# Two graph layers on one core: laying out buffers by when they end, and issuing the second layer's first loads among the first layer's last gathers

## Chip, cores, metric

One core of one Trainium2 chip runs the whole kernel. The metric is the device time of one execution in microseconds; lower is better. Engines are named as in the profile: PE (matrix multiply), PEld (its weight load), DVE (vector), ACT (scalar), POOL, and SP, which here only issues DMAs.

## What is computed

```python
h = relu(layernorm(x))                       # x: 2500 x 1024
x = x + segment_sum((h @ W0)[src] * edge_weight[:, None], dst)   # 80000 edges, sorted by dst
h = relu(layernorm(x)) @ W1.T + b1
deg = 1 + count(row == n)                    # row = src, col = dst, and a self edge per node
x = x + segment_sum(deg[row]**-0.5 * deg[col]**-0.5 * h[col], row)
```

## The kernel before

Nodes lie in 20 tiles of 128 (`NT`); the last has 68. `ORDER` gives the order in which tiles are finished. Arithmetic follows three stages.

**Support.** Each x tile is normed and multiplied by W0 (L282); the rows of `support` are stored to device memory. Meanwhile DVE and PE count the edges between tiles (`count_group`, L442 to L466): `counts` tiles are stored as `cnat`, and `total` adds them up for the degrees.

**Layer 1.** For the four thickest tiles (0 to 3), a `dense` weighted count matrix is multiplied with rows of `support` (`multiplied`, L632). For the 16 others `gathered` fetches, block by block, 128 edge rows with an indirect DMA issued on POOL (L592, eight `msg` buffers), makes a one-hot `oh_r`, splits the weighted message into `hi` on ACT (L598) and `lo` on DVE (L600), and adds four matmuls into `sums` (L604). When a tile's blocks are done, `finish` adds x (L562), stores x1 (L563), norms it (`normed`, L133 to L145) and transposes it on PE (L546) with copies to `vT` on ACT (L547). Then `second_rows` multiplies with W1 (L577; the profile has two PE records for each fp32 matmul), adds `bias` (L581) and stores `hid_d` (L584). A plan written out in Python interleaves blocks, dense rows and pieces of `finish` and `second_rows`; after the plan's end what is left is run off: first `preparing` and `waiting` (the last tiles' `finish`), then `products_left` (their `second_rows`).

**Layer 2.** Degrees are reduced (L740) and `dis` made (L743); a flag `missing` is computed that says whether a general fallback has to run (L744 to L754; one matmul of `ones` and `placed`, L749). Then each `hid_d` tile is loaded (`rows`, three buffers, L764), scaled by `dis` and split into `hi` (ACT, L766) and `lo` (DVE, L768), all kept in SBUF for all 20 tiles. For each output tile r, `counts_of` loads a transposed column of `cnat` with a DMA transpose on SP (`cT`, L774) and casts it to fp32r on ACT (`bT`, L776, two buffers); 80 matmuls (L794) run over all tiles in `ORDER`. Rows 0 and 1 are done as a pair, so that each fresh `hi`/`lo` serves two rows; the rest one by one. `row` loads x1 (L781), adds (L782) and stores (L784).

A scheduler at build time orders the instructions of each engine; buffers of one name rotate in program order. `order_behind` adds an edge to that ordering only, with no semaphore. Pools are stacked: a pool opened after others are closed takes their bytes. With `reuse_waits="tile"` a tile of such a pool waits for the earlier users of its own bytes (in PSUM, of its own bank) only; otherwise it waits for all users of the pools below it. `lay2`, `work2` and `psum2` of layer 2 have this already. They begin where `lay` began, so `hi` and `lo` of the first tiles in `ORDER` lie on `lay`'s tiles, `bias` among them.

Of the kernel before, what the change touches and what calls it, by code (L numbers as in the profile page):

```python
# [9 lines left out]
F32 = mybir.dt.float32  # L10
F32R = mybir.dt.float32r
# [28 lines left out]
OPENING = 8  # L40
BESIDE = 12
TAIL = 48

ORDER = (3, 4, 5, 6, 2, 7, 8, 9, 1, 10, 11, 12, 13, 0, 14, 15, 16, 17, 18, 19)

# [2 lines left out]
def direct(  # L48
# [67 lines left out]


    first = ctx.enter_context(ExitStack())
    lay = first.enter_context(tc.tile_pool(name="lay", bufs=1))
    work = first.enter_context(tc.tile_pool(name="work", bufs=2))  # L120
    psum = first.enter_context(tc.tile_pool(name="psum", bufs=2, space=bass.MemoryType.PSUM))
    ohs = first.enter_context(tc.tile_pool(name="ohs", bufs=8))
    cpool = first.enter_context(tc.tile_pool(name="cpool", bufs=3))
    wpool = first.enter_context(tc.tile_pool(name="wpool", bufs=1, reuse_waits="tile"))
    sup_ctx = tc.tile_pool(name="sup", bufs=4, side="right")
    sup = sup_ctx.__enter__()
    prep_ctx = tc.tile_pool(name="prep", bufs=1)
# [158 lines left out]

    def products(t):
        hT, rstd = ready.pop(t)
        mm = psum.tile([P, 2, H], F32, name="mm")
        yield from product(hT, w0_sb, mm)  # L290
        row = sup.tile([P, D], F32, name="row", bufs=2)
        nc.scalar.activation(row, mm.rearrange("p h d -> p (h d)"), AF.Copy, scale=rstd)
        nc.sync.dma_start(support[t * P:t * P + rows(t), :], row[:rows(t), :])
# [138 lines left out]
    def count_group(t, g, a, b):  # L432

        nonlocal last_count
        w = WINDOWS[t][1]
        cleared(t)
        if g % 4 == 0:
            bases[t] = nc.values_load_multi_w_load_instructions(
                base_i[0:1, g:g + 4], engines=[DVE], min_val=0, max_val=P - w,
                skip_runtime_bounds_check_because="a row of a tile")[1]  # L440
        v = bases[t][g % 4]
        cb = psum.tile([P, 512], F32, name="cb")  # L442
        ab = []
        for k in range(a, b):
            oh_low = ohs.tile([P, P], BF, name="oh_low")
            nc.vector.tensor_scalar(oh_low, iota16[:, :P], low[:, k:k + 1], None, op0=ALU.is_equal)  # L446
            oh_key = ohs.tile([P, KW], BF, name="oh_key")
            nc.vector.tensor_scalar(oh_key[:, :NT * w], iota16[:, :NT * w], key[:, k:k + 1], None,  # L448
                                    op0=ALU.is_equal)
            last_count = nc.tensor.matmul(  # L450
                cb[:, :NT * w], oh_low, oh_key[:, :NT * w], start=(k == a), stop=(k == b - 1))
            if t < DENSE:
                wl = ohs.tile([P, 3, P], BF, name="wl")
                for i in range(3):
                    nc.scalar.activation(wl[:, i, :], oh_low, AF.Copy, scale=wpart[:, i, k:k + 1])  # L455
                ab.append((wl, oh_key))
        to = counts[t][:, :, ds(v, w)]
        nc.vector.tensor_tensor(to, cb[:, :NT * w].rearrange("p (t w) -> p t w", w=w), to, op=ALU.add)  # L458
        if t < DENSE:
            for j, (wl, oh_key) in enumerate(ab):  # L460
                for i in range(3):
                    last_count = nc.tensor.matmul(  # L462
                        cb[:, 256:256 + NT * w], wl[:, i, :], oh_key[:, :NT * w],
                                     start=(j == 0 and i == 0), stop=(j == len(ab) - 1 and i == 2))
            to = dense[t][:, :, ds(v, w)]
            nc.vector.tensor_tensor(to, cb[:, 256:256 + NT * w].rearrange("p (t w) -> p t w", w=w), to,  # L466
                                    op=ALU.add)
        if b == K0[t + 1]:
            nc.vector.tensor_tensor(total, counts[t], total, op=ALU.add)
            to_store.append([6, t])  # L470
# [100 lines left out]
    def second_rows(t, vT):  # L571
# [12 lines left out]
        nc.sync.dma_start(hid_d[t], hid)  # L584
        yield 1.75, 0.65, 0.0

    def gathered(t, sums):
        n = TILE_BLOCKS[t]
        for j in range(n):
            k = K0[t] + j  # L590
            msg = gpool.tile([P, D], F32, name="msg", bufs=8)
            nc.gpsimd.indirect_dma_start(  # L592
                out=msg, out_offset=None, in_=support,
                in_offset=bass.IndirectOffsetOnAxis(ap=src_p[:, k:k + 1], axis=0))
            oh = gpool.tile([P, P], F32R, name="oh_r", bufs=3)
            nc.vector.tensor_scalar(oh, iota, row_p[:, k:k + 1], None, op0=ALU.is_equal)  # L596
            hi = gpool.tile([P, D], F32R, name="hi")
            nc.scalar.activation(hi, msg, AF.Copy, scale=wgt_p[:, k:k + 1])  # L598
            lo = gpool.tile([P, D], F32R, name="lo")
            nc.vector.scalar_tensor_tensor(lo, msg, wgt_p[:, k:k + 1], hi.bitcast(F32),  # L600
                                           op0=ALU.mult, op1=ALU.subtract)
            for v in (hi, lo):
                for h in range(2):
                    i = nc.tensor.matmul(  # L604
                        sums[:, h, :], oh, v[:, h * H:(h + 1) * H],
                        start=(j == 0 and v is hi), stop=(j == n - 1 and v is lo))
                    if v is hi and h == 0:
                        on_pe(i)
            yield 0.92, 1.47, 1.16
# [3 lines left out]
    def multiplied(ts):  # L613
# [3 lines left out]
        for t in ts:  # L617
            count_all(t)
        for h in range(2):
            sums = psum.tile([P, 2, H], F32, name="mm")  # L620
            cols = slice(h * H, (h + 1) * H)
            for k0 in range(0, NT, 2):
                msg = gpool.tile([P, 2, H], F32, name="msg", bufs=8)
# [52 lines left out]
    def blocks_of(tiles):  # L676
        nonlocal pending
        for t in tiles:
            sums = psum.tile([P, 2, H], F32, name="mm")
            for j, took in enumerate(gathered(t, sums)):  # L680
                if j == TILE_BLOCKS[t] - 1:
                    rest = finish(t, sums)
# [46 lines left out]
            count_next(queue)  # L729
    store_counts(late=False)  # L730
    assert not stored
    for rest in [preparing] * (preparing is not None) + waiting:
        for _ in rest:
            pass
    for rest in products_left:
        for _ in rest:
            pass


    nc.vector.tensor_reduce(deg, total, axis=mybir.AxisListType.X, op=ALU.add)  # L740
    nc.vector.tensor_scalar(dis, deg, 1.0, None, op0=ALU.max)
    nc.scalar.activation(dis, dis, AF.Sqrt)
    nc.vector.reciprocal(dis, dis)  # L743
    nc.vector.tensor_reduce(placed[:, 1:2], deg, axis=mybir.AxisListType.X, op=ALU.add)  # L744
    over = lay.tile([P, NT], F32, name="over")
    nc.vector.tensor_scalar(over, deg, 2048.0, None, op0=ALU.is_gt)
    nc.vector.tensor_reduce(placed[:, 2:3], over, axis=mybir.AxisListType.X, op=ALU.add)
    ps = psum.tile([P, 4, P], F32, name="pT")
    nc.tensor.matmul(ps[:, 0, :3], ones, placed, start=True, stop=True)  # L749
    lost = lay.tile([1, 3], F32, name="lost")  # L750
    for i, n in enumerate((E, E + N, 0)):
        nc.vector.tensor_scalar(lost[:, i:i + 1], ps[0:1, 0, i:i + 1], float(n), None, op0=ALU.not_equal)
    nc.vector.tensor_add(lost[:, 0:1], lost[:, 0:1], lost[:, 1:2])
    nc.vector.tensor_add(missing, lost[:, 0:1], lost[:, 2:3])  # L754
    first.close()


    lay = ctx.enter_context(tc.tile_pool(name="lay2", bufs=1, reuse_waits="tile"))
    work = ctx.enter_context(tc.tile_pool(name="work2", bufs=2, reuse_waits="tile"))
    psum = ctx.enter_context(tc.tile_pool(name="psum2", bufs=2, space=bass.MemoryType.PSUM, reuse_waits="tile"))  # L760
    his, los = {}, {}
    for t in ORDER:
        hf = work.tile([P, D], F32, name="rows", bufs=3)
        nc.sync.dma_start(hf, hid_d[t])  # L764
        his[t] = lay.tile([P, D], F32R, name=f"hi{t}")
        nc.scalar.activation(his[t], hf, AF.Copy, scale=dis[:, t:t + 1])  # L766
        los[t] = lay.tile([P, D], F32R, name=f"lo{t}")
        nc.vector.scalar_tensor_tensor(los[t], hf, dis[:, t:t + 1], his[t].bitcast(F32),  # L768
                                       op0=ALU.mult, op1=ALU.subtract)

    def counts_of(r):

        cT = work.tile([P, NT, P], F16, name="cT")
        nc.sync.dma_start_transpose(out=cT.rearrange("p t s -> p (t s)"), in_=cnat[r].rearrange("t p d -> (t p) d"))  # L774
        bT = work.tile([P, NT, P], F32R, name="bT")
        nc.scalar.copy(bT, cT)  # L776
        return bT
# [1 line left out]
    def row(r, mm):  # L779
# [3 lines left out]
                                       op0=ALU.mult, op1=ALU.add)  # L783
        nc.sync.dma_start(out[r * P:r * P + rows(r), :], xh[:rows(r), :])  # L784


    for rs in [(0, 1)] + [(r,) for r in range(2, NT)]:
        bTs = [counts_of(r) for r in rs]
        mms = [psum.tile([P, 2, H], F32, name="mm2", bufs=3) for r in rs]
        for k in ORDER:  # L790
            for bT, mm in zip(bTs, mms):
                for v in (his[k], los[k]):
                    for h in range(2):
# [2 lines left out]
                                         stop=(k == ORDER[-1] and v is los[k]))  # L796
        for r, mm in zip(rs, mms):
            row(r, mm)


def kernel(tc, edges, xT, *args):
# [338 lines left out]
```

## Time and profile before

| | |
|---|---|
| median of 3 runs | 1740.54 us (1735.3, 1740.54, 1742.44) |
| profiled execution | 1733.96 us, its span 1732.0 us |
| PE, DVE, ACT, POOL busy | 96%, 69%, 52%, 30% of the span |
| mean granted PE clock | 0.988 |
| last gather issued, last gather matmul ends | 1287.18, 1316.9 us |
| last product (L577) ends | about 1345.9 us |
| pair of rows 0 and 1 (L794) | 1346.91 to 1391.82 us |
| rows 2 to 19 (L794) | 1393.82 to about 1722.9 us |

The profile's timeline lists instructions in order of time with, in brackets, the idle time of the engine before them and what ended it. The chain of waits follows what released each step back from the end. The windows view gives busy times in stretches.

### The profile page before, as it was taken

How to read it: one execution, taken by the hardware profiler on the slowest of the kernel's cores; microseconds unless marked ns; L12 is line 12 of the kernel's file. 1: busy time of each engine (PE TensorE's matmuls, PEld its weight loads, DVE VectorE, ACT ScalarE, POOL GpSimd, SP SyncE). 2: the span in 40 equal slices, each digit the busy share in tenths (PEclk: the TensorE clock that was granted, in tenths of full speed). 3: DMA queues.
4: the chain of work that ended last, by engine and by line, in shares of the span. 5: the costliest groups of instructions: out<-in, count | busy, mean ns of one | idle time of the engine just before them, and what ended most of it. 6: DMA issues, size and time to landing. Idle time of an engine off the chain costs nothing. (4 is left out here: it accounts for less than half of the span.)

```text
span 1732.0 us, 21214 instructions
## 1 busy us (share of the span) xinstructions
PE 1654.1 (96%) x6506; PEld 1030.8 (60%) x6506; DVE 1200.3 (69%) x3051; ACT 907.9 (52%) x1476; POOL 525.6 (30%) x501
## 2 busy tenths in 40 slices
PE   6999999999999999999999999998999899999997
PEld 2466555554445555655555555654564678888886
DVE  5788888888889999999999999996772510000000
ACT  3399999982236765665555556664553421111110
POOL 3000000000057776775555556664530000000000
PEclk9999999999999999999999999999999999999999
DMA  7512212123399999998988899898875663433320
GB/s 249 188 62 65 89 53 60 54 68 92 79 364 330 384 317 323 331 362 281 308 286 282 282 322 331 318 333 297 264 265 134 210 164 91 107 79 105 93 65 32
DMA packets 213584, 351.57 MB, mean 203 GB/s; under 512 B 115354, under 2 KB 134820, under 8 KB 213462
## 3 DMA queue, kind: packets, MB, share of 16 engines
q0 software_dynamic: 60592, 219.74, 36.2%
q1 hardware_dynamic: 152870, 130.39, 24.8%
q8 instruction: 54, 0.88, 0.2%
q14 instruction: 68, 0.56, 0.1%
HBM read 282.41 MB, written 54.56 MB: 195 GB/s over the span
## 5 line engine op out<-in xcount | busy, mean ns | idle before, releaser
L598 ACT ACTIVATE hi<-msg,wgt_p 128x1024 fp32r<-128x1024 f32 x378 | 428.6, 1149 | 280.6 <-PE mm L604 180.4
L592 POOL DMA_INDIRECT msg<-support,src_p x378 | 478.0, 1265 | 293.6 <-DVE oh_r L596 90.0
L600 DVE SCALAR_TENSOR_TENSOR lo<-msg,wgt_p,hi 128x1024 fp32r<-128x1024 f32 x378 | 480.1, 1277 | 36.7 <-ACT hi L598 21.1
L604 PE MATMUL mm<-lo,oh_r 128*128 128x512 f32 x756 | 309.8, 491 | 13.2 <-DVE lo L600 13.0
L282 PE MATMUL mm<-w,hT 128*128 128x512 f32 x640 | 318.4, 609 | 2.4 <-ACT hT L174 2.4
L577 PE MATMUL pT<-w,vT 128*128 128x512 f32 x640 | 312.4, 597 | 0.0
L604 PE MATMUL mm<-hi,oh_r 128*128 128x512 f32 x756 | 273.5, 442 | 0.7 <-ACT hi L598 0.7
L455 ACT ACTIVATE wl<-oh_low,wpart 128x128 bf16<-128x128 bf16 x891 | 262.2, 420 | 0.0
L794 PE MATMUL mm<-hi,bT 128*128 128x512 f32 (+1 forms) x800 | 247.6, 392 | 4.6 <-ACT bT L776 2.0
L794 PE MATMUL mm<-lo,bT 128*128 128x512 f32 (+1 forms) x800 | 247.7, 392 | 3.3 <-DVE lo L768 3.3
L782 DVE SCALAR_TENSOR_TENSOR rows<-mm,dis,rows 128x1024 f32<-128x1024 f32 x20 | 25.7, 1283 | 307.9 <-PE mm L794 307.8
L604 PEld LDWEIGHTS mm<-lo,oh_r 128*128 128x128 f32 x756 | 137.9, 189 | 129.3 <-DVE lo L600 51.1
L448 DVE TENSOR_SCALAR oh_key<-iota,key 128x200 bf16<-128x200 f16 (+12 forms) x675 | 194.4, 290 | 5.0 <-PE cb L462 4.9
L776 ACT CAST bT<-cT 128x2560 fp32r<-128x2560 f16 x20 | 46.6, 2335 | 261.0 <-PE mm L794 257.7
L604 PEld LDWEIGHTS mm<-hi,oh_r 128*128 128x128 f32 x756 | 139.3, 189 | 64.2 <-issue 30.2
L794 PEld LDWEIGHTS mm<-hi,bT 128*128 128x128 f32 (+1 forms) x800 | 150.4, 189 | 37.9 <-ACT hi L766 3.1
L794 PEld LDWEIGHTS mm<-lo,bT 128*128 128x128 f32 (+1 forms) x800 | 150.0, 188 | 38.3 <-DVE lo L768 7.0
L458 DVE TENSOR_TENSOR counts<-cb,counts 128x200 f32 (+13 forms) x296 | 138.5, 469 | 48.0 <-PE cb L450 41.2
L446 DVE TENSOR_SCALAR oh_low<-iota,low 128x128 bf16<-128x128 f16 x675 | 167.2, 251 | 1.4 <-ACT wl L455 1.2
L632 PE MATMUL mm<-msg,dense 128*128 128x512 f32 (+1 forms) x320 | 157.1, 601 | 10.2 <-DMA msg<-support 10.2
L577 PEld LDWEIGHTS pT<-w,vT 128*128 128x128 f32 x640 | 120.9, 191 | 72.6 <-issue 55.5
L282 PEld LDWEIGHTS mm<-w,hT 128*128 128x128 f32 x640 | 109.1, 195 | 65.4 <-issue 59.2
(144 smaller groups left out, 1177.5 us busy)
## 6 DMA issues: line engine op xcount, KB each, us to landing
msg<-support POOLq DMA_DIRECT2D x36, 512.0 KB, 6.8
xt<-in_x SPq DMA_DIRECT2D x34, 512.0 KB, 7.3
cnat<-counts SPq DMA_DIRECT2D x20, 640.0 KB, 5.4
hid_d<-hn SPq DMA_DIRECT2D x20, 512.0 KB, 6.5
rows<-hid_d SPq DMA_DIRECT2D x20, 512.0 KB, 4.4
rows<-x_d SPq DMA_DIRECT2D x20, 512.0 KB, 3.8
hT<-in_xT SPq DMA_DIRECT2D x19, 512.0 KB, 3.7
support<-row SPq DMA_DIRECT2D x19, 512.0 KB, 2.9
```

The source lines that it names most:

```text
L282: on_pe(nc.tensor.matmul(mm[:, h, :], vT[:, k, :], ws[k][:, h * H:(h + 1) * H], start=(k == 0), stop=(k == KC - 1)))
L446: nc.vector.tensor_scalar(oh_low, iota16[:, :P], low[:, k:k + 1], None, op0=ALU.is_equal)
L448: nc.vector.tensor_scalar(oh_key[:, :NT * w], iota16[:, :NT * w], key[:, k:k + 1], None, op0=ALU.is_equal)
L455: nc.scalar.activation(wl[:, i, :], oh_low, AF.Copy, scale=wpart[:, i, k:k + 1])
L458: nc.vector.tensor_tensor(to, cb[:, :NT * w].rearrange("p (t w) -> p t w", w=w), to, op=ALU.add)
L577: on_pe(nc.tensor.matmul(mm, vT[:, k, :], w1_sb[k][:, h * H:(h + 1) * H], start=(k == 0), stop=(k == KC - 1)))
L592: nc.gpsimd.indirect_dma_start(out=msg, out_offset=None, in_=support, in_offset=bass.IndirectOffsetOnAxis(ap=src_p[:, k:k + 1], axis=0))
L598: nc.scalar.activation(hi, msg, AF.Copy, scale=wgt_p[:, k:k + 1])
L600: nc.vector.scalar_tensor_tensor(lo, msg, wgt_p[:, k:k + 1], hi.bitcast(F32), op0=ALU.mult, op1=ALU.subtract)
L604: i = nc.tensor.matmul(sums[:, h, :], oh, v[:, h * H:(h + 1) * H], start=(j == 0 and v is hi), stop=(j == n - 1 and v is lo))
L632: m = nc.tensor.matmul(sums[:, i, :], dense[t][:rows(k), k, :], msg[:rows(k), k - k0], start=(k == 0), stop=(k == NT - 1))
L794: nc.tensor.matmul(mm[:, h, :], bT[:rows(k), k, :], v[:rows(k), h * H:(h + 1) * H], start=(k == ORDER[0] and v is his[k]), stop=(k == ORDE ...
```

## The change

The SBUF pools `lay`, `work`, `ohs` and `cpool` get `reuse_waits="tile"`, and `wpool` moves ahead of `ohs` and `cpool`. The PSUM pool is split in three: `psum_c` (the `cb` tiles), `psum_m` (the `mm` tiles) and `psum` (the `pT` tiles), in this order. In layer 2, `psum2` is opened first; then come a pool `late` with the hi/lo of the 11 tiles last in `ORDER`, in reverse order, `work2`, and a pool `early` with the hi/lo of the first `EARLY = 9`. Splitting a tile becomes a function, called inside the loop of the first pair; its load is ordered behind one of the last gathers, and so are the transposing loads of `cnat`. After the plan's end, `products_left` is run off first, then the unfinished `finish`, then `products_left` again. The flag's reductions, matmul and comparisons move behind row 4.

```diff
+EARLY = 9
-    lay = first.enter_context(tc.tile_pool(name="lay", bufs=1))
-    work = first.enter_context(tc.tile_pool(name="work", bufs=2))
+    lay = first.enter_context(tc.tile_pool(name="lay", bufs=1, reuse_waits="tile"))
+    work = first.enter_context(tc.tile_pool(name="work", bufs=2, reuse_waits="tile"))
+    psum_c = first.enter_context(tc.tile_pool(name="psum_c", bufs=2, space=bass.MemoryType.PSUM))
+    psum_m = first.enter_context(tc.tile_pool(name="psum_m", bufs=2, space=bass.MemoryType.PSUM))
     psum = first.enter_context(tc.tile_pool(name="psum", bufs=2, space=bass.MemoryType.PSUM))
-    ohs = first.enter_context(tc.tile_pool(name="ohs", bufs=8))
-    cpool = first.enter_context(tc.tile_pool(name="cpool", bufs=3))
     wpool = first.enter_context(tc.tile_pool(name="wpool", bufs=1, reuse_waits="tile"))
+    ohs = first.enter_context(tc.tile_pool(name="ohs", bufs=8, reuse_waits="tile"))
+    cpool = first.enter_context(tc.tile_pool(name="cpool", bufs=3, reuse_waits="tile"))
...
+    drawn = []
     def gathered(t, sums):
...
-            nc.gpsimd.indirect_dma_start(
+            drawn.append(nc.gpsimd.indirect_dma_start(
                 out=msg, out_offset=None, in_=support,
-                in_offset=bass.IndirectOffsetOnAxis(ap=src_p[:, k:k + 1], axis=0))
+                in_offset=bass.IndirectOffsetOnAxis(ap=src_p[:, k:k + 1], axis=0)))
...
-    for rest in [preparing] * (preparing is not None) + waiting:
-        for _ in rest:
-            pass
-    for rest in products_left:
-        for _ in rest:
-            pass
+    def exhaust(generators):
+        while generators:
+            for _ in generators.pop(0):
+                pass
+    exhaust(products_left)
+    exhaust([preparing] * (preparing is not None) + waiting)
+    exhaust(products_left)
...
-    lay = ctx.enter_context(tc.tile_pool(name="lay2", bufs=1, reuse_waits="tile"))
+    psum = ctx.enter_context(tc.tile_pool(name="psum2", bufs=2, space=bass.MemoryType.PSUM, reuse_waits="tile"))
+    late = ctx.enter_context(tc.tile_pool(name="late", bufs=1, reuse_waits="tile"))
+    his, los = {}, {}
+    def parts_of(t, pool):
+        his[t] = pool.tile([P, D], F32R, name=f"hi{t}")
+        los[t] = pool.tile([P, D], F32R, name=f"lo{t}")
+    for t in ORDER[:EARLY - 1:-1]:
+        parts_of(t, late)
     work = ctx.enter_context(tc.tile_pool(name="work2", bufs=2, reuse_waits="tile"))
-    psum = ctx.enter_context(tc.tile_pool(name="psum2", bufs=2, space=bass.MemoryType.PSUM, reuse_waits="tile"))
-    his, los = {}, {}
-    for t in ORDER:
+    early = ctx.enter_context(tc.tile_pool(name="early", bufs=1, reuse_waits="tile"))
+    for t in ORDER[:EARLY]:
+        parts_of(t, early)
+    def split(t):
         hf = work.tile([P, D], F32, name="rows", bufs=3)
-        nc.sync.dma_start(hf, hid_d[t])
-        his[t] = lay.tile([P, D], F32R, name=f"hi{t}")
+        order_behind(nc.sync.dma_start(hf, hid_d[t]), drawn[-max(12 - 4 * ORDER.index(t), 1)])
         nc.scalar.activation(his[t], hf, AF.Copy, scale=dis[:, t:t + 1])
-        los[t] = lay.tile([P, D], F32R, name=f"lo{t}")
...
     def counts_of(r):
         cT = work.tile([P, NT, P], F16, name="cT")
-        nc.sync.dma_start_transpose(out=cT.rearrange("p t s -> p (t s)"), in_=cnat[r].rearrange("t p d -> (t p) d"))
+        i = nc.sync.dma_start_transpose(out=cT.rearrange("p t s -> p (t s)"),
+                                        in_=cnat[r].rearrange("t p d -> (t p) d"))
+        order_behind(i, drawn[-max(30 - 12 * r, 1)])
...
     for rs in [(0, 1)] + [(r,) for r in range(2, NT)]:
...
         for k in ORDER:
+            if rs[0] == 0:
+                split(k)
...
         for r, mm in zip(rs, mms):
             row(r, mm)
+        if rs[0] == 4:
+            all_placed()
```

`all_placed()` holds L744 to L754 as they were, with its matmul in an `mm2` tile of `psum2` and its small tiles in `keep`.

More of the change, by code (lines that the diff above doesn't have):

```diff
@@ L288, in products @@
         hT, rstd = ready.pop(t)
-        mm = psum.tile([P, 2, H], F32, name="mm")
+        mm = psum_m.tile([P, 2, H], F32, name="mm")
         yield from product(hT, w0_sb, mm)
@@ L441, in count_group @@
         v = bases[t][g % 4]
-        cb = psum.tile([P, 512], F32, name="cb")
+        cb = psum_c.tile([P, 512], F32, name="cb")
         ab = []
@@ L619, in multiplied @@
         for h in range(2):
-            sums = psum.tile([P, 2, H], F32, name="mm")
+            sums = psum_m.tile([P, 2, H], F32, name="mm")
             cols = slice(h * H, (h + 1) * H)
@@ L678, in blocks_of @@
         for t in tiles:
-            sums = psum.tile([P, 2, H], F32, name="mm")
+            sums = psum_m.tile([P, 2, H], F32, name="mm")
             for j, took in enumerate(gathered(t, sums)):
@@ L743, in direct @@
     nc.vector.reciprocal(dis, dis)
[L744 to L754, printed above, removed]
-    first.close()
-    lay = ctx.enter_context(tc.tile_pool(name="lay2", bufs=1, reuse_waits="tile"))
+    first.close()
+    psum = ctx.enter_context(tc.tile_pool(name="psum2", bufs=2, space=bass.MemoryType.PSUM, reuse_waits="tile"))
[6 more added lines that the diff above has]
+        parts_of(t, late)
     work = ctx.enter_context(tc.tile_pool(name="work2", bufs=2, reuse_waits="tile"))
-    psum = ctx.enter_context(tc.tile_pool(name="psum2", bufs=2, space=bass.MemoryType.PSUM, reuse_waits="tile"))
-    his, los = {}, {}
-    for t in ORDER:
+    early = ctx.enter_context(tc.tile_pool(name="early", bufs=1, reuse_waits="tile"))
+    for t in ORDER[:EARLY]:
+        parts_of(t, early)
+    def split(t):
         hf = work.tile([P, D], F32, name="rows", bufs=3)
-        nc.sync.dma_start(hf, hid_d[t])
-        his[t] = lay.tile([P, D], F32R, name=f"hi{t}")
+        order_behind(nc.sync.dma_start(hf, hid_d[t]), drawn[-max(12 - 4 * ORDER.index(t), 1)])
         nc.scalar.activation(his[t], hf, AF.Copy, scale=dis[:, t:t + 1])
-        los[t] = lay.tile([P, D], F32R, name=f"lo{t}")
         nc.vector.scalar_tensor_tensor(los[t], hf, dis[:, t:t + 1], his[t].bitcast(F32),
@@ L784, in row, with all_placed @@
         nc.sync.dma_start(out[r * P:r * P + rows(r), :], xh[:rows(r), :])
+    def all_placed():
+        nc.vector.tensor_reduce(placed[:, 1:2], deg, axis=mybir.AxisListType.X, op=ALU.add)
+        over = keep.tile([P, NT], F32, name="over")
+        nc.vector.tensor_scalar(over, deg, 2048.0, None, op0=ALU.is_gt)
+        nc.vector.tensor_reduce(placed[:, 2:3], over, axis=mybir.AxisListType.X, op=ALU.add)
+        ps = psum.tile([P, 2, H], F32, name="mm2", bufs=3)
+        nc.tensor.matmul(ps[:, 0, :3], ones, placed, start=True, stop=True)
+        lost = keep.tile([1, 3], F32, name="lost")
+        for i, n in enumerate((E, E + N, 0)):
+            nc.vector.tensor_scalar(lost[:, i:i + 1], ps[0:1, 0, i:i + 1], float(n), None, op0=ALU.not_equal)
+        nc.vector.tensor_add(lost[:, 0:1], lost[:, 0:1], lost[:, 1:2])
+        nc.vector.tensor_add(missing, lost[:, 0:1], lost[:, 2:3])
     for rs in [(0, 1)] + [(r,) for r in range(2, NT)]:
```

## The prediction

> **What bounds the kernel now.** I first read the page's busy shares: PE is at 96% of 1732.0 us, so a change can only pay where PE stands still or runs slowly. The windows then show where that is.
>
> ```profile
> 1250.00:1300.00 50.00, 50.00 (x173) 30.48 (x172) 39.36 (x60) 30.39 (x32) 20.87 (x19) 1.00 0.77 259
> 1319.00:1336.00 17.00, 13.63 (x34) 6.69 (x35) 2.30 (x6) 8.40 (x7) 0.00 (x0) 0.90 0.97 237
> 1348.00:1392.00 44.00, 39.05 (x157) 28.47 (x157) 24.96 (x21) 20.93 (x19) 0.00 (x0) 1.00 0.73 234
> 1400.00:1450.00 50.00, 50.00 (x222) 41.35 (x221) 2.57 (x2) 4.67 (x2) 0.00 (x0) 1.00 0.40 108
> ```
>
> Columns: stretch, length, busy PE, PEld, DVE, ACT, POOL, clock, DMA share, GB/s. PE is full in the last gathers and again once layer 2 runs row by row; the loss lies in the seam, 1317 to 1394. The PE timeline there:
>
> ```profile
> 1316.74 1.88 PE L577 MATMUL pT<-w,vT 128*128 128x512 f32 x4
> 1322.37 1.55 PE L546 MATMUL pT<-ident,hn 128*128 128x128 f32 x8 [3.75 <-ACT hn L145]
> 1323.74 22.11 PE L577 MATMUL pT<-w,vT 128*128 128x512 f32 x48
> 1345.68 0.28 PE L749 MATMUL pT<-placed,ones 128*128 128x3 f32 x2
> 1346.91 0.93 PE L794 MATMUL mm<-hi,bT 128*128 128x512 f32 x3 [0.94 <-DVE lost L753]
> ...
> 1390.61 1.21 PE L794 MATMUL mm<-lo,bT 68*128 68x512 f32 x4
> 1393.82 0.73 PE L794 MATMUL mm<-hi,bT 128*128 128x512 f32 x2 [2.00 <-ACT bT L776]
> ```
>
> PE waits 3.75 us for the last tile's norm; then the 48 products run, 16 of which (the second half of tile 18) needed no such norm. The first pair of layer-2 rows takes 1391.82 - 1346.91 = 44.91 us. The chain of waits gives the unhindered rates:
>
> ```profile
> 1309.90 1.72 PE pT L577 x4
> 1349.50 5.00 DMA rows<-hid_d
> 1357.10 5.43 DMA rows<-hid_d
> 1366.24 4.00 DMA rows<-hid_d
> 1393.82 329.04 PE mm L794 x1440
> ```
>
> So a product record costs 0.43 us, a layer-2 matmul 329.04/1440 = 0.2285 us, and the pair's 160 would need 36.56 us: it loses 8.35 us, because three `rows` buffers reload only as each `lo` is done. Why nothing was split earlier is in the waits of 1290 to 1395:
>
> ```profile
> ACT hi L766 <- DMA rows<-hid_d: 20.8, 15, 3.6
> ACT hi L766 <- DVE hn L581: 13.1, 1, 13.1
> ```
>
> The second is a buffer wait: L581 reads `bias`, whose bytes in `lay` lie under the first `lo` and second `hi` of layer 2, and it runs last at 1345.89. Only one `hi` (1332.35) escaped. Similarly the first L794 waited for `lost` (L753), the last reader of a `pT` bank.
>
> **What the skill says.** The Trainium skill, "Perfetto Trace Analysis", section "Tensor Engine Instruction", calls ACT and DVE strict FIFO. The trace agrees: at 1206.27 DVE's stats (L133) had waited 7.52 us for a load, and PE, needing the `lo` behind it, stood 6.00 us until 1208.40. "DMA: Bandwidth & Descriptors", section "Issuing engines are not separate DMA queues", says transfers from all issuers share the same 16 engines; here four transposes and two row loads raised the share to 0.97 in 1319 to 1336. "TensorE: Matmul & The Clock Gate", section "What's actually happening", says an idle window of about 3.4 us throttles PE's clock until it has been busy again. The trace agrees: after the 3.75 us gap the clock column falls to 0.90, and 48 records take 22.11 us, not 20.64.
>
> **The change, part by part** (times of the profiled execution).
>
> *Order of the tail.* Tile 18's remaining 16 records (6.9 us) now come before tile 19's norm and transposes. DVE's stats need only tile 19's sums, so the chain of about 5.4 us (1316.94 to 1322.37) runs beside them. Gone: 3.75 us idle, the slow clock (22.11 - 20.64 = 1.47) and the slow transposes (1.55 - 2 x 0.44 = 0.67, less 0.18 of overlap). Saved: 5.7 us. Late next: the two vT copies of 0.59 us; the first half is copied while the second is transposed, so I take nothing for them; they could cost at most 1.2.
>
> *Places of buffers.* Nine of twenty hi/lo pairs (72 KB a partition) move to the far end, on bytes of `dense` and the gather's msg, hi and lo; the other eleven, of the tiles needed last, go on `lay`, `work` and the weights. Layer 2's PSUM falls on the cb and mm banks, not pT. Tiles 3, 4, 5 can then be split before the gathers end, the next ones as msg buffers end (last gather issued 1287.18), and all nine by about 1325; PE turns them into 9 x 1.83 = 16.4 us of work after about 1340. The eleven late ones wait for the weights, free when the products end. Three are preloaded; the reload pace was (1383.9 - 1348.3)/17 = 2.1 us a row, so the last is ready about 1340 + 4 + 8 x 2.1 = 1361, while PE asks for it at 1340 + 19 x 1.83 = 1375. The 8.35 us go. If the order puts early layer-2 matmuls ahead of the last products, the late eleven start up to 13 us later and up to 3 us come back.
>
> *Moved issues.* The transposes of rows 0, 1 and 2 go behind the 30th, 18th and 6th last gather (issued 1223.98, 1251.65, 1275.51), three row loads behind the 12th, 8th and 4th last (1263.40, 1271.80, 1280.11), the rest behind the last. All stay on SP; POOL gets none. A transpose holds SP 2.2 to 5.0 us; behind it there stand hid_d and x1 stores and L152's loads, which are issued at least 19 us before DVE uses them and land in about 7, so 5 us are covered. DMA work: 14.9/4 = 3.7 us a transpose, so 11 us plus three loads of 2 us = 17, in 64 us of which 0.77 are taken: 15 us free. That is tight, but POOL runs up to eight msg buffers ahead. ACT gets two casts of 2.33 and seven `hi` of 1.15 (12.7 us), DVE seven `lo` of 1.28 (9 us), all moved forward, none added. In 1250 to 1300 ACT has 19.6 us idle and DVE 10.6, but in pieces: a cast of 2.33 in an ACT gap of 1.5 delays the next `hi` by about 0.9. Two casts and a few such splits give 1 to 3 us at PE. A head-of-line wait for a DMA costs up to 6.0 each by the L133 case. Bounds for the whole part: 0 (all hidden; no gain, since PE has no idle to fill there) to five such waits, 30 us. I take 3 us.
>
> *The flag.* Two reductions and a comparison of 0.17 us leave DVE's gather stage; a matmul of 0.28 us with small DVE steps goes behind row 4, where DVE is busy 2.57 of 50 us and three PSUM buffers rotate. In the seam this frees 0.11 + 0.94 = 1.05 us; at row 4 it costs 0.28. The 2.00 us wait for row 2's cast stays: two bT buffers are both in use by the pair.
>
> *Waits by tile on the first pools* land on nothing released before them: nothing, and no cover is needed.
>
> Ceiling: 5.7 + 1.05 + 8.35 = 15.1 us. Check: 1318.62 + 20.64 + 0.88 + 36.56 + 2.00 = 1378.7 against 1393.82. Less 3 for the gathers and 0.3 for row 4: **12 us**. The profiled execution took 1733.96 (span 1732.0 and 2 around it), giving 1722. It is 6.6 us under the median of the three runs, 1740.54, for which I forecast 1728.
>
> **Rivals.**
> 1. *The split does not really start early.* The static order puts `hi` and `lo` behind late work, or the nine early places prove as late as the old ones. Then only the tail's order and the flag pay, 5 to 7 us: about 1735. For it: three row buffers, SP's in-order waits. Against: dense and msg are visibly done by 1312, and ACT and DVE are nearly empty from 1312 to 1342.
> 2. *The gathers choke* (the slower side). ACT or DVE stands before a cast or a split whose DMA has not landed, and PE, in the stage where it is full, stands with it. Place: the two casts and first three row splits, 1224 to 1290; price 6.0 us each. It eats the whole gain at the third and passes 0.5% slower at the fourth; all five make +15: about 1756. For it: DMA at 0.77 already, landings of 4.5 to 7.0 us for transposes without gathers beside them, and the L133 case. Against: bT is needed 90 us later, so nothing forces the cast to be early in ACT's order, and only 16 ACT and DVE instructions are moved into 90 us.
> 3. *Half and half*: the seam closes but the gathers lose 6 to 9 us: about 1733, and some of this falls within 0.5%.
>
> **How the numbers follow.** A measurement of this kernel can tell about 0.5%, 8.7 us, from no change. My forecast with rival 3's better half gives a saving above that: 0.68. Rival 1 and the rest of 3: 0.21. Rival 2 beyond the threshold: 0.11. Predicted is the likeliest case, 1728; its own range is 1722 to 1735. The overall range 1719 to 1742 runs from the full ceiling, with the runs' own scatter of some 5 us below, to rival 1 and a mild rival 2.
>
> **What would show it.** Right: no 3.75 us gap before L546, 48 product records in about 20.7 us at full clock, the pair's 160 matmuls within 37 to 39 us, `hi` L766 no longer waiting for `hn` L581 and its first ones before 1290, and row 2's cast wait of 2 us still there. Wrong: new PE waits on `lo` or `hi` L600/L598 in 1224 to 1317 with ACT waiting for `cT` or `rows`; or the pair still near 45 us. The forecast fails if the gathers' end moves by over 6 us, or if the first-phase order before 1224 changes at all, which I take as untouched.

## The result, and the profile after

The changed kernel takes 1744.66 us (median of 20 runs, 1740.14 to 1759.58) against 1738.88 us before (20 runs, 1730.89 to 1742.89): ratio 1.0053, 95% interval 1.0035 to 1.0071. By the ratio it is slower by some 9 us, where 12 us less were forecast. The medians differ by only 5.8 us; the ratio lies near that of the means (1747.5 and 1738.1 us), which some longer runs of the changed kernel raise. Its profiled execution took 1743.8 us, with a span of 1741.6.

The windows view of the changed kernel (columns as above) shows two stretches of the last gathers, then the pair's. In the kernel before, PE filled the first and lost only the 3.75 us gap in the second:

```profile
1275.00:1300.00 25.00, 20.72 (x70) 12.10 (x68) 13.85 (x18) 8.59 (x9) 9.37 (x9) 1.00 1.25 159
1300.00:1325.00 25.00, 15.37 (x40) 8.02 (x40) 9.39 (x16) 8.69 (x9) 0.94 (x1) 0.73 1.04 233
1366.00:1403.00 37.00, 35.81 (x157) 29.11 (x155) 16.69 (x14) 14.52 (x12) 0.00 (x0) 1.00 0.53 171
```

PE stands still in the last gathers, and from 1275 the DMA engines are recorded as more than full (1.25: the recorded times of their packets add up to more than the stretch holds) while they move only 159 GB/s. PE's timeline has the waits; L611, L582, L551 and L822 are the old L604, L577, L546 and L794:

```profile
1264.13 0.73 PE L611 MATMUL mm<-hi,oh_r 128*128 128x512 f32 x2 [2.78 <-ACT hi L605]
1265.45 0.73 PE L611 MATMUL mm<-lo,oh_r 128*128 128x512 f32 x2 [0.59 <-DVE lo L607]
1309.50 1.22 PE L611 MATMUL mm<-hi,oh_r 128*128 128x512 f32 x2 [13.79 <-ACT hi L605]
1326.22 0.66 PE L551 MATMUL pT<-ident,hn 128*128 128x128 f32 x4 [1.25 <-DVE hn L586]
...
1341.17 0.63 PE L611 MATMUL mm<-lo,oh_r 128*128 128x512 f32 x2
1341.64 8.75 PE L582 MATMUL pT<-w,vT 128*128 128x512 f32 x20
1350.22 0.60 PE L551 MATMUL pT<-ident,hn 128*128 128x128 f32 x4
...
1352.63 14.00 PE L582 MATMUL pT<-w,vT 128*128 128x512 f32 x32
...
1403.32 1.22 PE L822 MATMUL mm<-hi,bT 128*128 128x512 f32 x2 [1.51 <-ACT bT L788]
```

The lower half is the seam, and it closed as forecast: no bracket stands before the last tile's transposes (1350.22), and the chain of waits gives the pair's run in one piece:

```profile
1366.63 34.29 PE mm L822 x151
```

The sum over both: the last gather matmul ends at 1341.8 instead of 1316.9, 24.9 us later; from there to row 2's first matmul it takes 1403.3 - 1341.8 = 61.5 us instead of 76.9, which is 15.4 less (15.1 forecast). Net +9.5, and the spans differ by 9.6. So the question is the 24.9 us. The waits in brackets make 18.4 of them (2.78 + 0.59 + 13.79 + 1.25), and 1.1 stand there before the first moved transpose (the same matmul comes at 1209.53 instead of 1208.40). What is left is in the main slow running after the waits: the clock column is 0.93 in 1250 to 1275 and 0.73 in 1300 to 1325. What ACT waited for there:

```profile
ACT hi L605 <- DMA msg<-support,src_p: 19.2, 2, 18.9
...
ACT bT L788 <- DMA cT<-cnat: 4.3, 1, 4.3
```

The first line is behind the 13.79 us, the second (row 1's cast) behind the 2.78 and 0.59. SP's timeline points to the cause (L784 is the transposing load, the old L774; the second number is how long its issue held SP):

```profile
1215.29 5.92 SPq L784 DMA_TRANSPOSE cT<-cnat  x1
...
1247.50 5.83 SPq L784 DMA_TRANSPOSE cT<-cnat  x1
...
1275.35 0.28 SPq L157 DMA_DIRECT2D xt<-in_x  x1
1275.72 0.34 SPq L776 DMA_DIRECT2D rows<-hid_d  x1
1276.12 18.79 SPq L784 DMA_TRANSPOSE cT<-cnat  x1
1294.96 0.80 SPq L776 DMA_DIRECT2D rows<-hid_d  x1
1295.86 1.45 SPq L568 DMA_DIRECT2D x_d<-xt  x1
1297.34 22.86 SPq L784 DMA_TRANSPOSE cT<-cnat  x1
1320.30 14.85 SPq L589 DMA_DIRECT2D hid_d<-hn  x2
```

The transposes of rows 0 and 1 held SP under 6 us; those of rows 2 and 3 held it 18.79 and 22.86 us, and gathers issued beside row 2's took up to 32.3 us to land, where 4.1 to 9.5 us were seen before. The PE wait of 1.25 us goes back, in the chain of waits, to a hid_d store that SP could issue only at 1320.30, after the second long hold.

The trace's packet records say what kind of work this was. A transpose is 2560 packets of 256 bytes. In the kernel before, those of the first four transposes, after the gathers, took 19 to 21 ns each on average. In the changed kernel those of rows 0 and 1 took 22 and 21 ns, spread over 3.5 and 6.6 us. Row 2's took 143 ns each, spread over 26.6 us, and in that time 479 packets of the gathers' queue passed, 18 a microsecond, where the 1461 packets of 1275 to 1300 in the kernel with all transposes late (below) make 58 a microsecond. Row 3's first packet came 2 us after row 2's last, so part of its long hold is row 2's; its own packets took 47 ns each, spread over 13.6 us.

### The profile page after: what moved, and what is told of

Its sections match the earlier page's. It is cut to its first block, busy times and chain, and to the rows that moved or that the text cites. A ratio compares the mean times of both kernels' runs of the same rounds, so it can differ in the third digit from the quotient of the medians.

```text
span 1741.6 us, 21197 instructions
## 1 busy us (share of the span) xinstructions
PE 1653.4 (95%) x6506; PEld 1034.8 (59%) x6506; DVE 1199.7 (69%) x3051; ACT 906.4 (52%) x1476; POOL 527.1 (30%) x501
## 5 line engine op out<-in xcount | busy, mean ns | idle before, releaser
L611 PE MATMUL mm<-lo,oh_r 128*128 128x512 f32 x756 | 312.1, 494 | 13.8 <-DVE lo L607 13.6
L582 PE MATMUL pT<-w,vT 128*128 128x512 f32 x640 | 313.7, 599 | 0.1
L611 PE MATMUL mm<-hi,oh_r 128*128 128x512 f32 x756 | 275.3, 445 | 17.5 <-ACT hi L605 17.5
L822 PE MATMUL mm<-hi,bT 128*128 128x512 f32 (+1 forms) x800 | 248.7, 392 | 1.5 <-ACT bT L788 1.5
L822 PE MATMUL mm<-lo,bT 128*128 128x512 f32 (+1 forms) x800 | 247.3, 390 | 0.0
L794 DVE SCALAR_TENSOR_TENSOR rows<-mm,dis,rows 128x1024 f32<-128x1024 f32 x20 | 25.6, 1284 | 316.6 <-PE mm L822 316.6
L611 PEld LDWEIGHTS mm<-lo,oh_r 128*128 128x128 f32 x756 | 138.4, 191 | 132.7 <-DVE lo L607 54.1
L611 PEld LDWEIGHTS mm<-hi,oh_r 128*128 128x128 f32 x756 | 140.0, 190 | 83.0 <-issue 30.7
L822 PEld LDWEIGHTS mm<-hi,bT 128*128 128x128 f32 (+1 forms) x800 | 150.6, 189 | 33.4 <-ACT bT L788 1.9
L822 PEld LDWEIGHTS mm<-lo,bT 128*128 128x128 f32 (+1 forms) x800 | 150.7, 188 | 31.9 <-issue 0.2
L582 PEld LDWEIGHTS pT<-w,vT 128*128 128x128 f32 x640 | 121.4, 191 | 73.0 <-issue 55.6
L455 PE MATMUL cb<-oh_key,oh_low 128*128 128x200 bf16 (+12 forms) x675 | 139.1, 287 | 9.2 <-DVE oh_key L453 5.8
```

What stands on the lines that cost most here:

```text
L455: last_count = nc.tensor.matmul(cb[:, :NT * w], oh_low, oh_key[:, :NT * w], start=(k == a), stop=(k == b - 1))
L582: on_pe(nc.tensor.matmul(mm, vT[:, k, :], w1_sb[k][:, h * H:(h + 1) * H], start=(k == 0), stop=(k == KC - 1)))
L611: i = nc.tensor.matmul(sums[:, h, :], oh, v[:, h * H:(h + 1) * H], start=(j == 0 and v is hi), stop=(j == n - 1 and v is lo))
L822: nc.tensor.matmul(mm[:, h, :], bT[:rows(k), k, :], v[:rows(k), h * H:(h + 1) * H], start=(k == ORDER[0] and v is his[k]), stop=(k == ORDE ...
```

## The experiments

Ratios are to the kernel before, run on the same chip, with 95% intervals. `drawn[-n]` is the n-th last gather and `stores[-1]` tile 19's x1 store, which SP issues once the gathers are done.

**1. Rows 2 and on transposed after the gathers.**

```diff
-        order_behind(i, drawn[-max(30 - 12 * r, 1)])
+        order_behind(i, drawn[-(30 - 12 * r)] if r < 2 else stores[-1])
```

> The transposing loads of rows 2 and 3 are ordered on SP behind tile 19's x1 store, that is behind the last gather; those of rows 0 and 1, the row loads, the tail's order, the pools and the flag stay as in the changed kernel. Theory S (a transpose among the last, densest gathers runs many times slower than elsewhere and holds up the gathers): the 18.8 and 22.9 us holds on SP shrink to 2 to 6 us, PE's 13.8 us wait for hi goes, and the kernel beats the one before by 9 to 14 us, ratio 0.992 to 0.995. Rival W (the mere extra DMA work among the gathers, row loads included, makes the gathers late): rows 0 and 1 and the row loads are still there, about half of the wait stays, ratio about 0.998 to 1.001. Rival O (SP's order or the tail's order, not the transposes): nothing changes, ratio 1.005.

Measured: 1727.26 us, ratio 0.9926 (0.9905 to 0.9947). SP's holds are 4.1 to 5.6 us, the 13.8 us wait is gone, and PE waits 2.08 + 0.59 us behind row 1's cast. The slowdown lay in two transposing loads; W and O fall.

**2. All transposes after the gathers.**

```diff
+        order_behind(i, stores[-1])
```

> All transposing loads are ordered on SP behind tile 19's x1 store; the rest as in the changed kernel. Theory S: like the one with two late, and the PE wait of 2.8 + 0.6 us behind row 0's cast goes too, 12 to 15 us under the kernel before, ratio 0.991 to 0.993, if two transposes of some 4 us each and their casts still come before the products end. Rival W: as good as or better than with two late by 5 us or more. Rival O: ratio 1.005 again.

Measured: 1725.68 us, ratio 0.9914 (0.9891 to 0.9937), 15 us less than before, about the ceiling that was forecast for the seam. The same stretch in the windows view:

```profile
1275.00:1300.00 25.00, 25.00 (x84) 14.82 (x83) 19.42 (x30) 13.77 (x14) 9.46 (x9) 1.00 0.88 307
```

PE is full and the DMA engines move 307 GB/s with less recorded busy time than at 159. The price is a new wait of 2.12 us for row 0's bT at 1332.

**3. The tail's order alone**, on the kernel before (`products_left` first, then the unfinished norm, then the rest).

> The kernel before with the tail's order alone: the products left over first, then the unfinished norm and transposes, then the last products. My sum said 5.7 us less (3.75 idle, 1.96 of slow clock), ratio 0.9967. If the last tile's norm chain is hidden but layer 2 then waits for its rows from an earlier start, part is given back: ratio 0.9967 to 1.000. If the tail's order is what hurt in the changed kernel: over 1.002.

Measured: 1731.23 us, ratio 0.9957 (0.9938 to 0.9976), 7.5 us less by the ratio; 5.7 was forecast and lies inside the interval. The 3.75 us gap shrinks to one of 0.35 between the two halves of the transposes, and the pair keeps its waits for rows. By these totals about half of experiment 2's gain is the tail's order, but the interval is wide. The profiled executions part it better: from the last gather matmul to row 2's first, the seam takes 72.2 us here, 76.9 before and 61.5 in the changed kernel. So the tail's order gives 4.7 us of the 15.4, and the places of the buffers and the flag, which no experiment parts, the other 10.7.

**4. One transpose at the bad place.** All late except row 0's, which stands where the change has row 2's.

```diff
+        order_behind(i, drawn[-6] if r == 0 else stores[-1])
```

> As the kernel with all transposes late, but row 0's transpose is put behind the 6th last gather, where the changed kernel has row 2's. Theory S by place: this first transpose, alone, holds SP for 15 to 20 us there and PE waits 10 us or more for hi; ratio about 1.000. Rival by count or row (only a third transpose, or a second in flight beside a late one, is slow): it holds SP for about 6 us as rows 0 and 1 did in the changed kernel, and the ratio is that of all late plus at most 0.002.

Measured: 1750.67 us, ratio 1.0049 (1.0032 to 1.0066). SP is held 17.84 us and PE waits 19.54 us for hi, as theory S said, though the ratio is worse than its 1.000. It is not a matter of row, count or a second transpose in flight. Who holds whom differs from the changed kernel; the waits of this one:

```profile
ACT bT L789 <- DMA cT<-cnat: 22.2, 1, 22.2
PEld mm L612 <- ACT hi L606: 20.8, 3, 20.4
PE mm L612 <- ACT hi L606: 19.5, 1, 19.5
```

Here row 0's cast stands in ACT's queue ahead of the next `hi`, so the late transpose stops PE through ACT. In the changed kernel row 2's cast comes after the pair, and the late gathers themselves stopped ACT.

**5. The same without row loads before the gathers end** (`split` ordered behind `stores[-1]`).

> Row 0's transpose stands behind the 6th last gather again, but no layer-2 row load is issued before the gathers end: all are ordered behind tile 19's x1 store. Theory G (the slow transpose comes of gathers in flight beside it): still held on SP for 15 us or more, PE waits over 10 us for hi, ratio 1.000 to 1.006. Rival L (it comes of the row load issued just ahead of it on SP's queue): about 6 us on SP, no wait for hi, ratio 0.990 to 0.994.

Measured: 1743.33 us, ratio 1.0032 (1.0021 to 1.0042); SP held 17.24 us, PE waiting 18.62. The row load ahead isn't needed: L falls.

**6 and 7. Row 0's transpose behind the 12th and the 24th last gather.**

> As all transposes late, but row 0's is behind the 12th last gather, with x1's store and an x load ahead of it. Theory G, where any gathers in flight do it: slow here too, held over 12 us, ratio over 0.998. Rival P (only the place behind the 6th last is bad, by what the queues hold just then; rows 0 and 1 of the changed kernel ran at 6 us behind the 30th and 18th): about 6 us, ratio 0.991 to 0.995.

> The same with row 0's transpose behind the 24th last gather, where the changed kernel has none. If gathers in flight decide: slow, ratio over 0.998. If it is a matter of whether the gather queue happens to be empty when the transpose starts: either is possible, and the hold on SP goes with the landing times of the gathers around it.

Measured: 1736.22 us, ratio 0.9992 (0.9977 to 1.0007), with SP held 11.94 us; and 1722.85 us, ratio 0.9936 (0.9911 to 0.9962), with SP held 7.97. The first is as theory G said, the second is not. In the first, PE's longest wait (9.73 us) is again for late gathers. The transposes of these profiled executions are the longer, the more packets of the gathers' queue pass meanwhile: 23.6 us with 557, 8.9 us with 179, and 2.7 to 4.8 us for the later ones with none. The runs of the second fall in two groups, 1720.91 to 1722.85 (four) and 1731.07 to 1735.13 (three). This fits a program that goes either way at one place, but only the fastest of them has a trace.

**8. Two transposes behind tile 17's store.** `second_rows` keeps its store in `hid_stores`.

```diff
+        order_behind(i, hid_stores[ORDER[-3]] if r < 2 else stores[-1])
```

> A version meant to be best: rows 0 and 1 transposed behind tile 17's hid_d store (about 1314, the last gather has landed), rows 2 and on behind tile 19's x1 store; all else as in the changed kernel. The 2.1 us that PE waited for row 0's bT with all late should go: 2 us under that kernel, ratio 0.990. If the transposes then collide with the last row loads or x1 stores and bT is no earlier: ratio 0.991 to 0.992.

Measured: 1721.34 us, ratio 0.9911 (0.9891 to 0.9931). The wait for row 0's bT is gone; up to the end of the pair PE's largest wait is 0.77 us, and row 2's cast still costs 1.51. The median lies 17 us under the kernel before, but the interval doesn't part it from experiment 2. PE's timeline and SP's:

```profile
1327.06 1.09 PE L551 MATMUL pT<-ident,hn 128*128 128x128 f32 x8 [0.77 <-ACT hn L150]
...
1379.27 0.73 PE L824 MATMUL mm<-hi,bT 128*128 128x512 f32 x2 [1.51 <-ACT bT L790]
```

```profile
1310.41 6.22 SPq L786 DMA_TRANSPOSE cT<-cnat  x2
```

Two transposes hold SP 6.22 us together, once the gathers have landed.

**9. Layer 2's x1 loads and output stores issued on POOL** (in experiment 8's kernel).

> The version with two transposes behind tile 17's store, but in layer 2 each row's x1 load and output store are issued on POOL instead of SP, so that plain 512 KB transfers run from POOL's queue beside the transposes of the later rows on SP. Theory Q (a transpose is slow whenever packets from another queue alternate with its own on the DMA engines): transposes that overlap them land in 8 us or more, against 6.4 before; PE has 20 us a row and should not notice, time within 5 us of that version. Rival (it takes gathers, row by row with indirect addresses): landings stay at 6 to 7 us.

Measured: one run, 1731.9 us (before 1740.6), more than the 5 us that were expected at most above experiment 8's 1721.34; why is open. From 1400 on SP's holds are 2.96 to 4.43 us, median 3.16, against 2.28 to 3.87 and 2.81 in experiment 8. The first transpose with POOL transfers beside it met 190 packets of their queue and took 5.9 us, against 4.0 for the same row in experiment 8. No landing was recorded for these. It settles little about Q: with plain transfers beside them no transpose was slow, but about as many packets among gathers (125 and 179) went with 6.6 and 8.9 us, and no plain stream as dense as the last gathers was tried.

**10. Experiment 8 with all row loads after the gathers.**

> The version with two transposes behind tile 17's store, with all row loads behind tile 19's x1 store instead of three among the last gathers. If the early loads are worth what the change meant: the pair starts later or starves, 3 to 6 us slower than that version, ratio about 0.993 to 0.995. If the places of the buffers do it all (the splits stood behind the gathers in ACT's order anyway): the same, ratio 0.990 to 0.992.

Measured: 1723.44 us, ratio 0.9902 (0.9886 to 0.9917). The early row loads bring nothing that can be measured, and without them the seam takes 61.7 us, with them 62.3 (experiment 8): what the seam gains comes from the tail's order, the places of the buffers and the flag.

**11. A plain load in place of the transpose.** Row 0's counts are loaded in 256-byte runs and not transposed.

```diff
+        if r == 0:
+            i = nc.sync.dma_start(cT, cnat[r].rearrange("t p d -> p t d"))
```

> As the kernel with row 0's transpose alone behind the 6th last gather, but that one load is a plain DMA of the same 640 KB in runs of 256 bytes, not a transpose, so row 0's counts are not transposed; all else is the same. Theory X (it is the transposing that is slow among gathers): the load lands in under 15 us, PE's wait for hi is under 3 us, ratio 0.990 to 0.995. Rival B (256-byte packets of any kind do it): held and late as with the transpose, ratio 1.003 to 1.005.

Measured: 1736.08 us, ratio 0.9972 (0.9962 to 0.9982), which neither X nor B gave. The load takes 21.8 us from issue to ACT's start on it, so ACT's cast waits 11.02 us and PE 8.32. But 1030 packets of the gathers' queue pass in its 17.6 us, 58 a microsecond: the gathers run on at their pace, though the load reads the same memory in the same small runs. So the slow arrival needs no transposing; that the gathers drop to a third was seen only with it. The one traced execution (1729.15 us) was the fastest of the 20, so how the slower ones went is not shown.

**12. Four `msg` buffers instead of eight** (experiment 4's kernel).

> As the kernel with row 0's transpose alone behind the 6th last gather, but with four msg buffers instead of eight, for the gathers and the dense loads, so that at most four gathers can be outstanding beside the transpose. If the backlog of gathers sets how long it takes: it is held on SP for under 10 us against 17.8, and PE's wait there is under half of 19.5. If a few gathers suffice: still over 14 us. The gathers themselves may be slower throughout, which the total time will show and which isn't counted here.

Measured: one run, 1952.35 us, slower throughout as allowed for; SP held 22.82 us, PE waiting 22.97. So the backlog does not decide it here: with at most four gathers outstanding it is as bad.

**13 and 14. Behind the 9th and the 10th last gather**: neighbours, the first right behind a load on SP's queue, the second behind a store.

> Row 0's transpose alone, behind the 9th last gather; on SP it comes right behind the last tile's x load (68 rows), as at the 6th last, but 0.5 us apart from it in time. Theory A (a load just ahead on SP's own queue makes a transpose among gathers slow; those behind a store ran in 6 us): held 12 us or more, PE waits over 5 us, ratio over 0.998. Theory P (place in time, the nearer the last gathers the worse): between the 12th last (11.9 us, 0.9992) and the 6th last (17.8 us, 1.0049).

> The same one gather earlier, behind the 10th last: now it comes on SP right behind a hid_d store and ahead of that x load, some 5 us earlier. Theory A: held for about 6 us, no long wait for hi, ratio 0.991 to 0.995. Theory P: as slow as behind the 9th last, 12 us or more, ratio over 0.998.

Measured: 1745.9 us, ratio 1.0035 (1.0021 to 1.0048); and 1738.33 us, ratio 0.9987 (0.9973 to 1.0001). The profiled executions show SP held 17.26 and only 6.88 us, but the second's cast still waited 16.67 us: a short hold on SP doesn't mean that the transpose is done. (That execution, 1745.8 us, was the slowest of its 20; the fastest was 1729.85.) Behind a store is better but not good: A falls as a rule. The ratios by place, from the 24th last to the 6th last (0.9936, 0.9992, 0.9987, 1.0035, 1.0049), lie closer to theory P.

**15. The changed kernel with row 2's transpose moved to the 10th last**, rows 3 and on after the gathers.

> The changed kernel with row 2's transpose behind the 10th last gather (behind a store) instead of the 6th last (behind two loads), and those of rows 3 and on behind tile 19's x1 store; rows 0 and 1 as changed. Theory A: no transposing over 8 us, ratio 0.992 to 0.995. Theory P: row 2 still slow, ratio 0.999 to 1.003.

Measured: 1739.42 us, ratio 0.9994 (0.9971 to 1.0018), runs from 1728.95 to 1749.42. In the profiled execution, one of the slowest, row 0's transpose, behind the 30th last gather and with the same instructions before it on SP as in the changed kernel, held SP 8.27 us instead of 5.92 and cost PE a wait. Its packets were spread over 15.5 us, against 3.5 in the changed kernel and 3.1 in experiment 1, which have it at the same place:

```profile
1222.49 8.27 SPq L785 DMA_TRANSPOSE cT<-cnat  x1
```

```profile
1247.83 1.22 PE L612 MATMUL mm<-hi,oh_r 128*128 128x512 f32 x2 [8.32 <-ACT hi L606]
```

The time is as theory P said, not as A. No place among these gathers was shown to be safe: one and the same place is harmless in one execution and slow in another, and the loss is worse near the end.

**What stays open.** What happens inside the DMA engines, and why it comes oftener near the last gathers; also whether it takes gathers at all or any other stream as dense (9), and whether a transpose issued on another queue than SP's would fare the same, which was not tried. The backlog of gathers (12) and the neighbour on SP's queue (5, 13, 14) don't decide it; the count of gather packets met goes with the transpose's length, but that is also its consequence.

## Why the prediction was wrong, point by point

- **Tail's order**: right. The 3.75 us gap is gone, and alone it gave 7.5 us by the totals and 4.7 in the profiled seam (5.7 forecast).
- **Places of buffers and the pair**: right in size. The 151 matmuls recorded in one piece took 34.29 us, the seam became 15.4 us shorter (15.1 forecast, tail and flag included). It is no matter of one execution: in experiments 1 and 4 to 15 the seam takes 61.5 to 63.0 us (65.1 in experiment 2, where PE waits for row 0's bT). Wrong in one detail: the first `hi` of layer 2 came at 1335.4, not before 1290, since ACT's order has them behind the gathers' own. The seam shows no cost of it, and experiment 10 shows that loading three rows early wasn't needed.
- **Flag**: right. Its matmul at row 4 takes 0.12 us of the chain, and `lost` holds up no L822.
- **Row 2's cast wait**: still there, 1.51 us for 2.00.
- **Moved issues**: the step that failed. It was put at 3 us; the gathers' end moved by 24.9. The term that was mis-sized is the transpose among gathers: "14.9/4 = 3.7 us a transpose" was taken from a stretch with no gather in it (14.90 us is how long four issues held SP there; the packets of each were done in 2.6 to 3.3) and added to the gathers' share as if DMA work only added up. Row 2's was spread over 26.6 us and cut the gathers to a third. The bound "A transpose holds SP 2.2 to 5.0 us", from the same stretch, fell with it (18.79 and 22.86).
- **Waits by tile on the first pools**: not tested alone. Both kernels are 1.1 us apart at 1209.
- **Rival 2** named the place and the sign. Its mechanism, a cast in ACT's queue whose DMA has not landed, cost 2.78 + 0.59 us in the changed kernel (row 1's) and far more than its 6.0 us a case in experiments 4, 5, 13 and 14 (19.54 in the first). But most of the changed kernel's loss came another way: the gathers' own landings were late, 13.79 us in one wait. **Rival 3** had the shape, a closed seam and slower gathers, with 6 to 9 us where 24.9 came.
- The chance of 0.11 for slower rested on "bT is needed 90 us later". That says nothing of what the transfer does to its neighbours meanwhile.

The sum for the moved issues was also short of room. Its 17 us of moved work did not fit into the 15 us that it called free, and the share of 0.77 behind these 15 is that of 1250 to 1300, in which the gathers end (the last is issued at 1287.18). In the kernel before, 1225 to 1250 shows a DMA share of 0.86, and then:

```profile
1250.00:1275.00 25.00, 25.00 (x93) 15.93 (x92) 21.20 (x32) 17.29 (x19) 15.04 (x13) 1.00 0.89 301
```

So some 6 of these 50 us were free (an estimate from the two shares). Lack of room alone is not the cause, though. Experiment 1 keeps two transposes and the row loads there, experiment 11 loads the same bytes at a bad place, and both are faster than the kernel before.

The best versions here keep the change's places, flag and tail and leave the transposes until the gathers have landed: 0.9902 to 0.9914 in experiments 2, 8 and 10.

## What to carry to other kernels

A transfer moved forward into a stage that waits on other transfers has to be priced in that stage, by kind and not by bytes; a duration from an empty stretch is only a lower bound. When a change joins several moves, hold the sum of each move against its own stretch of the profile: here one stretch gained 15 us and its neighbour lost 25. A wide scatter of runs (19 us against 12 before) may be the first sign of a transfer that goes well only by chance; here that is argued, since only one run of each kernel has a trace.

## What the runs showed of the hardware

A DMA transpose of 640 KB took 2.4 to 4.8 us when POOL's queue moved nothing (307 of them in these traces), its 256-byte packets 18 to 37 ns on average. Among indirect gathers it took from 3.5 us to 26.6 in the changed kernel alone, with packets of 22 and 143 ns. During the slow one the gathers fell from 58 to 18 packets a microsecond, and to 12 to 24 during those of experiments 4, 5, 6, 13 and 14; the engines' busy share read 1.25 at 159 GB/s against 0.88 at 307. A plain load in 256-byte runs at the same place arrived late too (21.8 us), but left the gathers at 58. The Trainium skill, "DMA: Bandwidth & Descriptors", section "Rules for kernel authors", says that a transpose next to ordinary DMAs needs nothing; it speaks there of what has to be kept apart to be safe, and these runs show a cost in time that it doesn't mention. SP can be held long by such a transpose (18.79 us, row 2's in the changed kernel) or let go early (6.88 us of some 25, experiment 14), so the time on the queue alone doesn't price it.
